# Deferring ten tiles' output products of a sparse graph attention kernel past its last q, k, v product, with deeper gathers and layer norm's small steps on VectorE

## The chip, the cores and the metric

The kernel runs on one core of a Trainium2 chip. Times are device microseconds of that core. Each is one run of the whole program, and runs are compared by their medians.

## The reference

There are 16 graphs (B) of 1024 nodes with 512 features, float32, and one adjacency matrix of 1024 x 1024 zeros and ones for all of them. Node degrees are very uneven: the first nodes have up to some tens of neighbours, the last ones few.

```python
q = (x @ Wq + bq).reshape(b, n, H, HD)     # H = 8 heads of HD = 64
k = (x @ Wk + bk).reshape(b, n, H, HD)
v = (x @ Wv + bv).reshape(b, n, H, HD)
scores = jnp.einsum('bqhd,bkhd->bhqk', q, k) / jnp.sqrt(jnp.float32(HD))
scores = scores + (1.0 - adj)[None, None, :, :] * -1000000000.0
attn = jax.nn.softmax(scores, axis=-1)
out = jnp.einsum('bhqk,bkhd->bqhd', attn, v).reshape(b, n, d)
y = x + out @ Wo + bo
return (y - mean(y)) / sqrt(var(y) + 1e-5)
```

## The kernel before

The kernel uses that the matrix is sparse. Once, at the start, it turns the adjacency matrix into lists of edges (`edges`). A tile is 128 query nodes of one graph, so there are 8 tiles in a graph and 128 in all. For each tile the edges are cut into blocks of 128 pairs of a query and a key. The first OWN[t] blocks hold one neighbour for each of the tile's queries, and the remaining BLOCKS[t] blocks hold the surplus edges of the queries with many neighbours. That makes 12, 5, 4, 3, 3, 3, 3, 3 blocks for tiles 0 to 7, 36 for a graph (NB) and 576 in the whole run. A tile is written (b, t) below: (13, 0) is tile 0 of graph 13.

There are three kinds of work.

1. *Products of q, k, v* (called `fronts` in the code): x is loaded and transposed, and `pair` makes q (L465) and k, v (L581, with seven products for the four quadrants of two tiles), which go to DRAM tables of rows, `q_rows` and `kv_rows`. A last row holds the mean of v. When it is written, the graph counts as set up (L531).
2. *Blocks of attention.* `gather` fetches, with indirect DMAs that GpSimd issues, the k and v rows of a block's keys (L695), and for a surplus block its q rows too (L690). For the other blocks q comes with one load for each tile (L684). VectorE multiplies q and k (L712) and adds up over each head (L716), ScalarE takes the exponential (L726), and ScalarE (L736) or VectorE (L740) weighs v. Own blocks are added up by VectorE (L752), surplus blocks by TensorE with a 0/1 matrix (L761, L762). `normalise` divides (L768 to L775), TensorE transposes the result (L780) and ScalarE copies it to oT (L784).
3. *Finishing a tile.* `load_y` loads x again into y (L637), two turns later GpSimd adds bo (L638), `product` multiplies oT by Wo on TensorE (L465, "po"), and VectorE adds it to y with a row sum (L647). Layer norm follows: a centre step on VectorE (L650), the square sum on ScalarE (L654), scale, power and shift on GpSimd (L657 to L659), and the normalised y on ScalarE (L662) with the store (L663).

All engines run their instructions in the order in which this loop writes them. One turn n of the loop is one block: gathers are issued for block n + 8 (AHEAD, L867), L712 and L716 for block n + 4, the exponential for n + 3, weighing for n + 1 or n + 2, sums for n. `later(k, fn)` puts a step k turns on, `later_last` the same at the end of that turn. TensorE's long work is rationed: every turn earns a `share` of its time (L862, computed once for each graph), every product unit costs its PRODUCT = 0.86 us, and units are taken while credit is positive, `finishing` before `fronts` (L893 to L900). A tile is finished when more than LAZY = 2 tiles wait while fronts are left, and at once afterwards, with at most one tile in two turns. With this the products of q, k, v are used up in turn 526, and from there to turn 576 only blocks and finishing remain. Fifty turns and the drain behind them make the end of the run.

SP issues all plain loads and stores in the order of the loop, so that a store which waits for its y holds up the loads behind it. A buffer that is used again makes its next load wait until the old content has been stored. y has four buffers.

`guard` (L795) starts at turn 540. It tests whether the edge lists and the size of the scores allow this method. Three powers on GpSimd (L817 to L819) come in it, then a few steps on VectorE (L821 to L826), whose result decides at the end of the run whether a dense routine (`tile_general`) has to run. With these inputs it doesn't.

Of the kernel before, what the change touches and what calls it, by code (L numbers as in the profile page):

```python
# [9 lines left out]
F32 = mybir.dt.float32  # L10
# [3 lines left out]
OP = mybir.AluOpType  # L14
# [3 lines left out]
EPS = 1e-5  # L18
# [9 lines left out]
AHEAD = 8  # L28
KG_BUFS, QG_BUFS, QT_BUFS, PV_BUFS = 8, 4, 3, 5
NO_ROW = 65536.0  # L30

LAZY = 2

ROWS = 3
EARLY = 11
LEAD_IN = 34
# [3 lines left out]
SUM = 0.87  # L40
TRANSPOSE = 0.44
LEAD_SHARE = 3.45

P = 128

# [102 lines left out]
def kernel(  # L148
# [34 lines left out]
    nc = tc.nc  # L183
    B, N, D = x.shape
    HD = D // HEADS
    NPAIR = D // P
    NT = N // P
# [4 lines left out]
    NS = sum(BLOCKS)  # L192
    NB = NS + sum(OWN)
# [11 lines left out]
    bo_bc = const.tile([P, D], F32, name="bo_bc")  # L205
# [8 lines left out]
    with ExitStack() as main:  # L214
        one = main.enter_context(tc.tile_pool(name="one", bufs=1))
        work = main.enter_context(tc.tile_pool(name="work", bufs=1))
        small = main.enter_context(tc.tile_pool(name="small", bufs=4))
        psum = main.enter_context(tc.tile_pool(name="psum", bufs=1, space=bass.MemoryType.PSUM))
        dram = main.enter_context(tc.tile_pool(name="dram", bufs=1, space=bass.MemoryType.DRAM))
# [34 lines left out]

        kv_rows = [dram.tile([N + 1, 2 * D], F32, name=f"kv_rows_{i}") for i in range(ROWS)]
        q_rows = [dram.tile([N, D], F32, name=f"q_rows_{i}") for i in range(ROWS)]
        zero = work.tile([1, D], F32, tag="q", name="zero", bufs=2)
        nc.gpsimd.memset(zero, 0.0)
        bias_rows = one.tile([2 * NPAIR, P], F32, name="bias_rows")
# [163 lines left out]
        X, XT, SX, KV, VSUM, NRM, Y, OT, PS = {}, {}, {}, {}, {}, {}, {}, {}, {}  # L423
        set_up = {}
# [206 lines left out]

        loaded = {}

        def load_y(b, t):
            Y[b, t] = work.tile([P, D], F32, tag="y", name=f"y_{b}_{t}", bufs=4)
            loaded[b, t] = now[0]
            nc.sync.dma_start(Y[b, t], x[b, ds(t * P, P), :])  # L637
            later(2, lambda: nc.gpsimd.tensor_tensor(Y[b, t], Y[b, t], bo_bc, op=OP.add))  # L638

        def finish(b, t):  # L640

            def out(p):
                OT.pop((b, t))
                y = Y[b, t]

                st = small.tile([P, 5], F32, name="stats", bufs=6)
                nc.vector.scalar_tensor_tensor(y, p, 1.0, y, op0=OP.mult, op1=OP.add, accum_out=st[:, 0:1])  # L647

                def centre():
                    nc.vector.tensor_scalar(st[:, 1:2], st[:, 0:1], -1.0 / D, None, op0=OP.mult)  # L650

                def spread():
                    sq = work.tile([P, D], F32, tag="ysq", name=f"ysq_{b}_{t}", bufs=1)
                    nc.scalar.activation(sq, y, AF.Square, bias=st[:, 1:2], accum_out=st[:, 2:3])  # L654

                def root():
                    nc.gpsimd.tensor_scalar(st[:, 2:3], st[:, 2:3], 1.0 / D, EPS, op0=OP.mult, op1=OP.add)  # L657
                    nc.gpsimd.tensor_tensor(st[:, 3:4], st[:, 2:3], neg_half, op=OP.pow)  # L658
                    nc.gpsimd.tensor_tensor(st[:, 4:5], st[:, 3:4], st[:, 1:2], op=OP.mult)  # L659

                def norm_out():
                    nc.scalar.activation(y, y, AF.Identity, bias=st[:, 4:5], scale=st[:, 3:4])  # L662
                    nc.sync.dma_start(out_ap[b, ds(t * P, P), :], y)  # L663
                    del Y[b, t]

                later(1, centre)
                later_last(1, spread)
                later(2, root)
                later_last(4, norm_out)

            out_ap = out_dram
            return product(f"po_{b}_{t}", lambda: OT[b, t], W["o"], out)


# [5 lines left out]
        def gather(n):  # L680
            b, t, i = blocks[n]
            if i == 0:
                QT[b, t] = work.tile([P, D], F32, tag="qt", name=f"qt_{b}_{t}", bufs=QT_BUFS)
                nc.sync.dma_start(QT[b, t], q_rows[b % ROWS][ds(t * P, P), :])  # L684
            if i < OWN[t]:
                g = NS + own[t] + i
            else:
                g = first[t] + i - OWN[t]
                QG[n] = work.tile([P, D], F32, tag="qg", name=f"qg_{n}", bufs=QG_BUFS)
# [4 lines left out]
            KG[n] = work.tile([P, 2 * D], F32, tag="kvg", name=f"kvg_{n}", bufs=KG_BUFS)  # L694
# [69 lines left out]
        def normalise(b, t):  # L764
            s, pv = PSUM.pop((b, t)), PV.pop((b, t))
            o = work.tile([P, D], F32, tag="o", name=f"o_{b}_{t}", bufs=2)
            r = small.tile([P, HEADS], F32, tag="rden", name=f"rden_{b}_{t}", bufs=2)
            nc.vector.tensor_tensor(r, s[:, 1, HD2:HD2 + HEADS], pv[:, D:], op=OP.add)  # L768
            nc.vector.tensor_tensor(  # L769
                o.rearrange("p (a d) -> p a d", a=2), s[:, :, 0:HD2], pv[:, 0:D].rearrange("p (a d) -> p a d", a=2),  # L770
                op=OP.add,
            )
            nc.vector.reciprocal(r, r)
            o8 = o.rearrange("p (h d) -> p h d", d=HD)
            nc.vector.tensor_tensor(o8, o8, r[:, :, None].to_broadcast([P, HEADS, HD]), op=OP.mult)  # L775

            def transpose():
                p = fill_psum(f"poT_{b}_{t}")
                for c in range(NPAIR):
                    nc.tensor.transpose(p[:, ts(c, P)], o[:, ts(c, P)], ident)  # L780

                def out():
                    OT[b, t] = work.tile([P, D], F32, tag="oT", name=f"oT_{b}_{t}", bufs=LAZY + 2)
                    nc.scalar.copy(OT[b, t], p)  # L784
                    later(1, lambda: done.append((b, t)))

                later(1, out)

            later(1, lambda: urgent.append(transpose))
            if not fronts:  # L790
                coming.append((b, t))
# [3 lines left out]
        def guard():  # L795
# [15 lines left out]
            r = small.tile([1, 8], F32, name="r")  # L811
            nc.vector.tensor_copy(r[:, 0:4], pg[0:1, 0:4])
            yield

            half = neg_half[0:1, 0:1]
            for i in (0, 1, 3):
                nc.gpsimd.tensor_scalar(r[:, i:i + 1], r[:, i:i + 1], 1e-30, None, op0=OP.max)  # L817
                nc.gpsimd.tensor_tensor(r[:, 4 + i:5 + i], r[:, i:i + 1], half, op=OP.pow)
                nc.gpsimd.tensor_tensor(r[:, i:i + 1], r[:, i:i + 1], r[:, 4 + i:5 + i], op=OP.mult)  # L819
            yield  # L820
            nc.vector.tensor_tensor(r[:, 4:5], r[:, 1:2], r[:, 3:4], op=OP.add)  # L821
            nc.vector.tensor_tensor(r[:, 4:5], r[:, 4:5], r[:, 0:1], op=OP.mult)
# [6 lines left out]
        done, coming, gathered, fronts = [], [], [0], []  # L829

        for i in range(KG_BUFS):
            nc.gpsimd.memset(work.tile([P, 2 * D], F32, tag="kvg", name=f"kvg_first_{i}", bufs=KG_BUFS), 0.0)
# [4 lines left out]
            prep.setdefault(EDGES_FROM[t], []).append(edges(t))  # L837
        prep.setdefault(12 - LEAD_IN, []).append(bias_setup())
        preps = [loads()]
        prep.setdefault((B - 1) * NB, []).append(guard())  # L840
        with tc.manual_schedule():

            fronts += transpose_x(0, 0) + transpose_x(0, 1)
# [5 lines left out]
            finishing, last_finish = [], -LEAD_IN  # L849
            credit = 0.0  # L850
            for t in range(3):
                load_x(0, t)
            n = -LEAD_IN
            while n < total or plan or rest or urgent or done or finishing:
                now[0] = n
                if n < 0:
                    share = LEAD_SHARE if n > -LEAD_IN else TRANSPOSE * 1.5
                elif n % NB == 0:

                    left = sum(u[0] for u in fronts)  # L860
                    goal = fronts_time - (n // NB + 2 + EARLY / NB) * batch_time
                    share = (max(0.0, left - goal) + NT * NPAIR * PRODUCT + NS * SUM) / NB  # L862
                if 0 <= n + 3 < total:
                    exponentials(n + 3)
                if 0 <= n + 4 < total:
                    products(n + 4)
# [87 lines left out]
```

## Time and profile before

| | us |
|---|---|
| median of 3 runs | 2127.69 |
| lowest, highest | 2127.08, 2128.05 |
| the profiled execution | 2129.36 |
| its span in the trace | 2127.5 |
| busy in the span: TensorE | 2038.1 (96%) |
| VectorE | 1850.6 (87%) |
| ScalarE | 1642.1 (77%) |
| GpSimd | 1278.5 (60%) |

The span is the time from the first to the last instruction of one profiled execution. An engine's busy time is the time in which at least one of its instructions was running. PE is TensorE's matmuls, PEld its weight loads, DVE VectorE, ACT ScalarE, POOL GpSimd and SP the engine that issues plain transfers. PEclk is the share of its full clock that TensorE was granted, and DMA the mean busy share of the 16 DMA engines. In a list of waits a line such as "DVE y L647 <- POOL y L638: 10.0, 5, 3.0" says that VectorE stood 10.0 us in all, 5 times, at most 3.0 us, before the instructions of L647, and that GpSimd's L638 ended most of it. The name "po<-wo,oT" gives what is written and what is read.

### The profile page before, as it was taken

The page shows a single profiled execution, that of the slowest core. Times are in us where ns is not written, and L with a number is a line of the kernel's source. Part 1 is how long each engine was busy: PE and PEld are TensorE (multiplying, and loading weights), DVE is VectorE, ACT ScalarE, POOL GpSimd, SP SyncE. Part 2 cuts the span into 40 slices and gives each one's busy share as a digit, 9 for nine tenths or more (in the row PEclk, how much of TensorE's full clock was granted, in tenths as well). Part 3 has the DMA queues.
Part 4 walks back from the last instruction along what each step waited for, and adds up shares of the span by engine and source line. Part 5 has one row for each costly group of instructions (what it writes and reads, how often), then busy time and mean ns, then how long its engine had stood idle before and what let it go on. Part 6 is the DMA issues. An engine that isn't in the chain of part 4 may idle for free. (4 is left out here: it accounts for less than half of the span.)

```text
span 2127.5 us, 29475 instructions
## 1 busy us (share of the span) xinstructions
PE 2038.1 (96%) x5933; PEld 1034.5 (49%) x5933; DVE 1850.6 (87%) x3592; ACT 1642.1 (77%) x8132; POOL 1278.5 (60%) x1366
## 2 busy tenths in 40 slices
PE   8897999999999999999999999999999999999746
PEld 3444555554555555455555545555554555545323
DVE  6789999988888888888898889988889888898866
ACT  4577887878878687787868788786878868697755
POOL 2034576756657575665756566575656656565775
PEclk9998999999999999999999999999999999999859
DMA  5267788887879788787978879787887879788774
GB/s 193 100 242 239 261 292 314 299 299 262 319 242 335 262 275 310 269 305 253 314 269 276 312 252 327 251 314 271 278 308 256 323 246 318 267 276 283 239 257 159
DMA packets 216716, 578.00 MB, mean 272 GB/s; under 512 B 33727, under 2 KB 33739, under 8 KB 216526
## 3 DMA queue, kind: packets, MB, share of 16 engines
q0 software_dynamic: 102144, 331.89, 46.7%
q1 hardware_dynamic: 111776, 239.16, 31.1%
q10 hardware_dynamic: 2606, 4.99, 0.7%
q14 instruction: 141, 1.16, 0.2%
q8 instruction: 49, 0.80, 0.2%
HBM read 474.75 MB, written 134.26 MB: 286 GB/s over the span
## 5 line engine op out<-in xcount | busy, mean ns | idle before, releaser
L695 POOL DMA_INDIRECT kvg<-kv_rows,key_row x576 | 629.5, 1093 | 395.2 <-ACT pv L726 109.9
L736 ACT ACTIVATE pv<-kvg,pv 128x64 f32<-128x64 f32 x2624 | 660.6, 338 | 0.0
L465 PE MATMUL pq<-wq,xT 128*128 128x512 f32 x1024 | 481.3, 595 | 0.0
L465 PE MATMUL po<-wo,oT 128*128 128x512 f32 x1024 | 471.9, 601 | 5.2 <-ACT oT L784 5.2
L716 DVE TENSOR_REDUCE s<-qk 128x8 f32<-128x512 f32 x576 | 391.3, 679 | 6.6
L690 POOL DMA_INDIRECT qg<-q_rows,query_row x240 | 274.7, 1144 | 76.7 <-issue 61.5
L465 PEld LDWEIGHTS po<-wo,oT 128*128 128x128 f32 x1024 | 196.2, 193 | 228.2 <-issue 206.7
L465 PEld LDWEIGHTS pq<-wq,xT 128*128 128x128 f32 x1024 | 189.6, 191 | 193.6 <-issue 178.8
L477 ACT ACTIVATE sq<-q 128x64 f32<-128x64 f32 x1024 | 245.5, 244 | 18.5 <-DVE q L492 18.3
L477 ACT ACTIVATE sq<-kv 128x64 f32<-128x64 f32 x1024 | 245.1, 243 | 1.0 <-DVE kv L604 0.6
L712 DVE TENSOR_TENSOR qk<-qt,kvg 128x512 f32<-128x512 f32 x336 | 243.7, 725 | 0.0
L581 PE MATMUL x<-b,xT 128*128 128x512 f32 x504 | 238.5, 596 | 0.1
L581 PE MATMUL pp<-t,s 128*128 128x512 f32 x504 | 237.2, 593 | 0.7 <-DVE w L597 0.7
L638 POOL TENSOR_TENSOR y<-y,bo_bc 128x512 f32<-128x512 f32 x128 | 173.2, 1353 | 100.0 <-DMA y<-in_x_dram 99.1
L477 ACT ACTIVATION_READ_ACCUMULATOR sq<-q 128x1 f32 x1024 | 195.1, 190 | 0.0
L477 ACT ACTIVATION_READ_ACCUMULATOR sq<-kv 128x1 f32 x1024 | 194.6, 190 | 0.0
L712 DVE TENSOR_TENSOR qk<-qg,kvg 128x512 f32<-128x512 f32 x240 | 173.8, 724 | 19.0 <-DMA kvg<-kv_rows,key_row 18.2
L761 PE MATMUL sum<-pv,sums 128*128 128x256 f32 x480 | 148.5, 392 | 26.1 <-DVE pv L740 23.5
L740 DVE TENSOR_TENSOR pv<-kvg,pv 128x512 f32<-128x512 f32 x248 | 170.5, 688 | 2.0 <-ACT pv L726 1.0
L726 ACT ACTIVATE pv<-s,absent 128x8 f32<-128x8 f32 x336 | 95.0, 292 | 94.8 <-DVE o L769 73.8
L647 DVE SCALAR_TENSOR_TENSOR y<-po,y 128x512 f32<-128x512 f32 x128 | 87.6, 684 | 81.4 <-POOL y L638 66.3
L761 PEld LDWEIGHTS sum<-pv,sums 128*128 128x128 f32 x480 | 91.3, 194 | 134.8 <-issue 99.6
(144 smaller groups left out, 3009.8 us busy)
## 6 DMA issues: line engine op xcount, KB each, us to landing
kv_rows<-kv SPq DMA_DIRECT2D x128, 512.0 KB
x<-in_x_dram SPq DMA_DIRECT2D x128, 256.0 KB
q_rows<-q SPq DMA_DIRECT2D x128, 256.0 KB
qt<-q_rows SPq DMA_DIRECT2D x128, 256.0 KB
y<-in_x_dram SPq DMA_DIRECT2D x128, 256.0 KB
out_dram<-y SPq DMA_DIRECT2D x128, 256.0 KB
kvg<-kv_rows,key_row POOLq DMA_INDIRECT x576
a<-in_adj_dram SPq DMA_DIRECT2D x8, 512.0 KB
```

The source lines that it names most:

```text
L465: nc.tensor.matmul(p, lhs()[:, ts(c, P)], w[:, c, :], start=(c == 0), stop=(c == NPAIR - 1))
L477: nc.scalar.activation(sq, s[:, ts(h, HD)], AF.Square, accum_out=NRM[b][:, i, t, h:h + 1])
L581: nc.tensor.matmul(R[bank], l[:, ts(c, P)], right[:, c, :], start=(first and c == 0), stop=(c == 1), skip_group_check=True,)
L638: later(2, lambda: nc.gpsimd.tensor_tensor(Y[b, t], Y[b, t], bo_bc, op=OP.add))
L690: nc.gpsimd.indirect_dma_start(out=QG[n], out_offset=None, in_=q_rows[b % ROWS], in_offset=bass.IndirectOffsetOnAxis(ap=query_row[:, g:g + ...
L695: nc.gpsimd.indirect_dma_start(out=KG[n], out_offset=None, in_=kv_rows[b % ROWS], in_offset=bass.IndirectOffsetOnAxis(ap=key_row[:, g:g + ...
L712: nc.vector.tensor_tensor(QK[n], q, KG[n][:, 0:D], op=OP.mult)
L716: nc.vector.tensor_reduce(S[n], QK.pop(n).rearrange("p (h d) -> p h d", d=HD), axis=AX.X, op=OP.add)
L726: nc.scalar.activation(PV[n][:, D:], S.pop(n), AF.Exp, bias=bias)
L736: nc.scalar.activation(pv[:, ts(h, HD)], v[:, ds(D + h * HD, HD)], AF.Copy, scale=pv[:, D + h:D + h + 1])
L740: nc.vector.tensor_tensor(pv[:, 0:D].rearrange("p (h d) -> p h d", d=HD), v[:, D:].rearrange("p (h d) -> p h d", d=HD), pv[:, D:, None].to ...
L761: nc.tensor.matmul(PSUM[b, t][:, 0, 0:HD2], m, pv[:, 0:HD2], **kw)
```

## The change

- The ten tiles (12, 6) to (13, 7), numbers 102 to 111, aren't finished in their turn. Their oT is stored to DRAM (`spill`). From the time that no `fronts` are left they are read back one after the other, at most two of them with a y at a time and at least three turns apart, into the buffers "e", "w", "g" of the q, k, v products, with y in the buffers "q".
- From graph 13 on, the share is computed anew in every turn so that the fronts end at turn 526 (EARLY and 3 turns before graph 15), and it is 3.0 after them.
- After the fronts gathers run 11 blocks ahead instead of 8. Every second q and k, v gather, and q of the even tiles, then take buffers that the fronts have left ("x", "xT", "kv").
- Layer norm's scale step (`variance`) and `shift` go from GpSimd to VectorE, for all tiles. The power stays on GpSimd, and shift comes a turn later.
- y + bo of even tiles goes to VectorE for tiles loaded after the fronts.
- The guard starts four turns earlier and leaves more turns between its steps.

```diff
+SPILL = range(102, 112)
+AHEAD_LAST = 11
+LAST_SHARE = 3.0
...
-        def load_y(b, t):
-            Y[b, t] = work.tile([P, D], F32, tag="y", name=f"y_{b}_{t}", bufs=4)
+        def load_y(b, t, tag="y", bufs=4):
+            Y[b, t] = work.tile([P, D], F32, tag=tag, name=f"y_{b}_{t}", bufs=bufs)
             loaded[b, t] = now[0]
             nc.sync.dma_start(Y[b, t], x[b, ds(t * P, P), :])
-            later(2, lambda: nc.gpsimd.tensor_tensor(Y[b, t], Y[b, t], bo_bc, op=OP.add))
+            engine = nc.gpsimd if fronts or t % 2 else nc.vector
+            later(2, lambda: engine.tensor_tensor(Y[b, t], Y[b, t], bo_bc, op=OP.add))
+
+        def reload(b, t, k):
+            OT[b, t] = work.tile([P, D], F32, tag="ewg"[k % 3], name=f"oTs_{b}_{t}", bufs=1)
+            nc.sync.dma_start(OT[b, t], spill[b * NT + t - SPILL[0]])
+            load_y(b, t, "q", 2)
+            later(2, lambda: done.append((b, t)))
...
-                def root():
-                    nc.gpsimd.tensor_scalar(st[:, 2:3], st[:, 2:3], 1.0 / D, EPS, op0=OP.mult, op1=OP.add)
+                def variance():
+                    nc.vector.tensor_scalar(st[:, 2:3], st[:, 2:3], 1.0 / D, EPS, op0=OP.mult, op1=OP.add)
                     nc.gpsimd.tensor_tensor(st[:, 3:4], st[:, 2:3], neg_half, op=OP.pow)
-                    nc.gpsimd.tensor_tensor(st[:, 4:5], st[:, 3:4], st[:, 1:2], op=OP.mult)
+
+                def shift():
+                    nc.vector.tensor_tensor(st[:, 4:5], st[:, 3:4], st[:, 1:2], op=OP.mult)
...
-                later(2, root)
+                later(2, variance)
+                later(3, shift)
                 later_last(4, norm_out)
...
-                QT[b, t] = work.tile([P, D], F32, tag="qt", name=f"qt_{b}_{t}", bufs=QT_BUFS)
+                tag, bufs = ("qt", QT_BUFS) if fronts or t % 2 else ("x", 3)
+                QT[b, t] = work.tile([P, D], F32, tag=tag, name=f"qt_{b}_{t}", bufs=bufs)
...
+                tag, bufs = ("qg", QG_BUFS) if fronts or i % 2 else ("xT", 4)
...
+            tag, bufs = ("kvg", KG_BUFS) if fronts or n % 5 % 2 == 0 else ("kv", 5)
...
                     nc.scalar.copy(OT[b, t], p)
-                    later(1, lambda: done.append((b, t)))
+                    if b * NT + t in SPILL:
+                        nc.sync.dma_start(spill[b * NT + t - SPILL[0]], OT.pop((b, t)))
+                        spilled.append((b, t))
+                    else:
+                        later(1, lambda: done.append((b, t)))
...
-        prep.setdefault((B - 1) * NB, []).append(guard())
+        prep.setdefault((B - 1) * NB - 4, []).append(guard())
...
+            fronts_end = (B - 1) * NB - EARLY - 3
...
+                elif n >= SPILL[0] // NT * NB + NB:
+
+                    share = sum(u[0] for u in fronts) / max(fronts_end - n, 1) + NS * SUM / NB if fronts else LAST_SHARE
...
-                while gathered[0] < min(n + AHEAD + 1, total) and blocks[gathered[0]][0] in set_up:
+                while gathered[0] < min(n + (AHEAD if fronts else AHEAD_LAST) + 1, total) and blocks[gathered[0]][0] in set_up:
...
-                    if tile_done not in loaded and len(Y) < 4:
+                    if tile_done not in loaded and sum(b * NT + t not in SPILL for b, t in Y) < 4:
                         load_y(*tile_done)
...
+                if spilled and not fronts and n > last_reload + 2 and sum(b * NT + t in SPILL for b, t in Y) < 2:
+                    reload(*spilled.pop(0), reloads)
+                    reloads, last_reload = reloads + 1, n
```

More of the change, by code (lines that the diff above doesn't have):

```diff
@@ L256 @@
         q_rows = [dram.tile([N, D], F32, name=f"q_rows_{i}") for i in range(ROWS)]
+        spill = [dram.tile([P, D], F32, name=f"spill_{i}") for i in range(len(SPILL))]
         zero = work.tile([1, D], F32, tag="q", name="zero", bufs=2)
@@ L688, in gather @@
                 g = first[t] + i - OWN[t]
-                QG[n] = work.tile([P, D], F32, tag="qg", name=f"qg_{n}", bufs=QG_BUFS)
+                tag, bufs = ("qg", QG_BUFS) if fronts or i % 2 else ("xT", 4)
+                QG[n] = work.tile([P, D], F32, tag=tag, name=f"qg_{n}", bufs=bufs)
                 nc.gpsimd.indirect_dma_start(
@@ L693, in gather @@
                 )
-            KG[n] = work.tile([P, 2 * D], F32, tag="kvg", name=f"kvg_{n}", bufs=KG_BUFS)
+            tag, bufs = ("kvg", KG_BUFS) if fronts or n % 5 % 2 == 0 else ("kv", 5)
+            KG[n] = work.tile([P, 2 * D], F32, tag=tag, name=f"kvg_{n}", bufs=bufs)
             nc.gpsimd.indirect_dma_start(
@@ L813, in guard @@
             yield
+            yield
             half = neg_half[0:1, 0:1]
@@ L819, in guard @@
                 nc.gpsimd.tensor_tensor(r[:, i:i + 1], r[:, i:i + 1], r[:, 4 + i:5 + i], op=OP.mult)
+            yield
+            yield
             yield
@@ L828 @@
         out_dram = out
-        done, coming, gathered, fronts = [], [], [0], []
+        done, coming, spilled, gathered, fronts = [], [], [], [0], []
         for i in range(KG_BUFS):
@@ L848 @@
             batch_time = fronts_time / B
-            finishing, last_finish = [], -LEAD_IN
+            finishing, last_finish, reloads, last_reload = [], -LEAD_IN, 0, 0
+            fronts_end = (B - 1) * NB - EARLY - 3
             credit = 0.0
@@ L853 @@
             n = -LEAD_IN
-            while n < total or plan or rest or urgent or done or finishing:
+            while n < total or plan or rest or urgent or done or finishing or spilled:
                 now[0] = n
```

## The prediction

> **What bounds the kernel now.** I read the busy row of the page first, then busy time by stretch, then who waits for whom in the stretches that the change touches, then single instructions there. I cut the span at VectorE's products of queries and keys (L712), because each of the 576 blocks has exactly one, written four turns ahead: turn 468 (first of batch 13) starts at 1761.1 us, turn 526 at 1958.7, turn 571 at 2100.6.
>
> ```profile
> PE   8897999999999999999999999999999999999746
> DVE  6789999988888888888898889988889888898866
> ```
>
> TensorE is full in nearly every slice and drops only in the last three. The stretches, with columns length, busy time of PE, PEld, DVE, ACT, POOL, granted clock, DMA share, GB/s:
>
> ```profile
> core 0: us, PE busy (x) PEld busy (x) DVE busy (x) ACT busy (x) POOL busy (x), PEclk, DMA share, GB/s
> ...
> 159.00:500.00 341.00, 328.45 (x963) 168.81 (x964) 320.73 (x633) 274.79 (x1361) 209.18 (x216) 0.97 0.83 283
> 500.00:1761.10 1261.10, 1260.55 (x3712) 643.00 (x3711) 1110.82 (x2129) 1008.51 (x5096) 792.09 (x842) 1.00 0.82 285
> 1761.10:1958.70 197.60, 197.60 (x576) 100.63 (x575) 175.42 (x329) 162.36 (x826) 123.88 (x133) 1.00 0.83 287
> 1958.70:2100.60 141.90, 93.90 (x246) 47.56 (x244) 112.11 (x226) 90.44 (x351) 104.83 (x121) 0.80 0.74 249
> 2100.60:2127.50 26.90, 14.52 (x44) 6.98 (x44) 10.87 (x27) 12.10 (x33) 8.34 (x15) 0.86 0.20 72
> ```
>
> Up to 1958.7 us TensorE is the bound: 197.60 busy of 197.60, with VectorE second at 89%. I call 1761.1 to 1958.7 stretch A. In 1958.7 to 2100.6 (stretch B) the products of q, k, v have run out, no engine is full, and TensorE idles 48 us. The last 26.9 us (C) drain. VectorE's waits in B:
>
> ```profile
> DVE y L647 <- POOL y L638: 10.0, 5, 3.0
> DVE qk L712 <- DMA kvg<-kv_rows,key_row: 8.6, 3, 4.1
> DVE r L821 <- POOL r L819: 6.0, 1, 6.0
> DVE y L647 <- issue: 2.6, 1, 2.6
> ```
>
> These are 27 of its 29.8 us of idle time: the addition of po waits for GpSimd's y + bo, gathers land late, and the guard waits for three powers on GpSimd. The chain that ended last covers only the last microseconds (statistics, y, store) and says nothing about A or B.
>
> **What the Trainium skill says.** "TensorE: Matmul & The Clock Gate", What's actually happening: the clock is throttled by default and activity releases it. The trace agrees. Eight po matmul records in a full stretch, and eight after idling in B:
>
> ```profile
> 1966.66 3.60 PE L465 MATMUL po<-wo,oT 128*128 128x512 f32 x8
> 1970.10 0.60 PE L761 MATMUL sum<-pv,sums 128*128 128x256 f32 x2
> ...
> 2004.62 6.78 PE L465 MATMUL po<-wo,oT 128*128 128x512 f32 x8 [1.00 <-ACT oT L784]
> ```
>
> "DMA: Bandwidth & Descriptors", Anatomy of one DMA — SWDGE (gpsimd) path: DMA engines don't wait on semaphores, the issuing sequencer does, and a transfer has about 2 us of fixed cost (measured there on the gpsimd path). Here SP indeed stands 51.5 us in B before output stores that wait for ScalarE's y, and a y load takes 2.7 us from issue to use when the DMA is idle (2106.3 to 2109.0) but 6.0 when it isn't (1997.3 to 2003.3). "SBUF — State Buffer", SBUF: two separate sides: a VectorE operation with two SBUF inputs and a GpSimd operation that reads SBUF exclude each other. The trace agrees: L712 at 1977.32 took 2.40 us instead of 0.68 while a y + bo ran on GpSimd.
>
> **Part 1: ten output products leave A.** The ten tiles (12,6) to (13,7) no longer get their product with Wo in A. One product is the eight records above: 1970.10 - 1966.66 = 3.44 us, so ten are 34.4 us, and A's TensorE time falls from 197.6 to 163.2. The products of q, k, v end in turn 525 either way, since the new share is made for that. VectorE loses ten additions (0.61 from start to next) and ten centre steps (0.06): 6.7 us, leaving 168.7. So VectorE takes over as the bound of A. ScalarE loses 10 x 1.5 us (147 left), GpSimd ten y + bo and statistics. DMA: 0.83 x 197.6 = 164 us of full use; ten y loads and ten stores go, ten spill stores come, 2.6 MB less of 56.7, so 156.5, or 0.90 of 174. Single windows of 12.4 us show 0.95 at 354 GB/s, so I take it as hidden; if not, A keeps a few us. To 168.7 I add waits. Before, VectorE waited 15.7 us in A for TensorE's products; with TensorE no longer full I keep a third, 5.3. A = 174.0, with ends 169 (no wait kept) and 184 (all 15.7 kept). Gain 23.6. The spill's store waits on SP for ScalarE's copy of oT; queued behind it are q, kv and x transfers, but the copy is issued in the same turn, so nothing is added; if ScalarE lagged a turn, the 3 us fall on transfers with several turns in hand.
>
> **Part 2: they come back in B.** In the built order of instructions, VectorE gets from turn 526 to 571: 9 more additions of po (0.61), 11 y + bo for even tiles (0.60 as L712 is spaced), 30 more small scalar steps and 21 shifts (0.06 to 0.08 each): 5.5 + 6.6 + 3.3 = 15.4, so 127.5 busy. With full single durations it would be 133. TensorE gets 9 x 3.4 = 31 us: 125, some of it at the lower clock, which should now rise as gaps close. DMA gets a spill read, a y load and a store for nine tiles, 6.9 MB on 35.3: 0.74 x 141.9 = 105 becomes 126. GpSimd stays near 104: more powers, but fewer y + bo and two small steps less for each tile. Three resources within 3% of each other don't all stay full, so B is VectorE's work plus waits:
> - guard: starts four turns earlier with four more turns of room, 6.0 to 0;
> - gathers: 11 ahead where the key row is used four turns early, so seven turns of lead for four, at some 3 us each. That is 21 us for 12, against an issue-to-use time that ran short at 5 to 8 us. 8.6 becomes 2. The first must still wait for the mean's row, as before;
> - y + bo on GpSimd, odd tiles only: 12.6 becomes 4;
> - new: VectorE itself waits for the y load of even tiles, with the next qk and the products with v queued behind, and TensorE's sums behind those. GpSimd waited 10.3 us in B for 13 loads, 0.8 each; VectorE reaches the place 2.2 to 5.9 us after the load's issue in turns 525 to 540, and up to 4 us before a landing of 6.0, but later has 6.8 us and more. Bounds 0 and 3.5 each; I take 1.3, so 11 x 1.3 = 14.
> B = 127.5 + 0 + 2 + 4 + 14 = 147.5, 5.6 more than before. SP's reloads of oT into the e, w, g buffers wait for the product of three reloads before, long done.
>
> **Part 3: layer norm's small steps on VectorE, all 128 tiles.** Up to 1761.1 they cost 100 x 2 x 0.07 = 14 us of VectorE, which has 150 us idle after 500 alone: hidden by TensorE. The wait counts more. `variance` waits for ScalarE's square sum, `shift` for GpSimd's power. Putting each where the new order has it between the instructions of the old trace, VectorE would arrive too early 33 times in the first 100 tiles, 52.7 us in total, at most 2.7, and 12.4 us for `shift`. Behind it stand scores and evacuations. But TensorE starts its sums at least 1.9 us after VectorE's weighting ends and the transpose of o at least 1.75 after o; only the part above 1.75, 7.1 us in total, could reach it, and VectorE already has waits of 2.95 us in this stretch with TensorE full. I take 1 us; ends -1 (GpSimd is freed) and 7. In C the chain gets two crossings between engines for two same-engine steps (POOL to POOL was 0.04 to 0.08), one more addition and 13 small steps: 28.0 for 26.9.
>
> **The sum.** 1761.1 + 1 + 174.0 + 147.5 + 28.0 = 2111.6 us of span against 2127.5: 15.9 less. The profiled execution took 2129.36, 1.9 more than its span, and lies 1.7 above the median of 2127.69, so I subtract from the median: 2111.8.
>
> **The rivals.**
> - *Both stretches at VectorE's rate.* Waits shrink once gathers lead: A 171, B 127.5 + 8 = 135.5, C 27.5, nothing before: 2095.1, so 2095.3. For it: VectorE already ran at 94% beside TensorE's 96% from 159 to 500. Against: DMA above 0.9 in both.
> - *Slower: VectorE held up by y's load.* Mechanism: y + bo of even tiles in B, in order on VectorE, behind a load that SP issues only after a store waiting for ScalarE. If each waits 3.5 us (6.0 to landing less 2.5 to arrival, as at tiles (14,4) and (14,6)), B grows by 11 x 2.2 = 24: 2136. It turns the sign from 1.3 + 15.9/11 = 2.75 us a tile. Against: most arrivals before came later than 4 us after issue.
> - *Given back, no change: layer norm's waits reach TensorE.* If a quarter of the 65 us of `variance` and `shift` waits passed on, 16 us go: 2128. Against: the lead of 1.75 us and more.
> - *The change not doing what it says* is excluded for the order: built, 40 po matmuls read reloaded tiles, after the last product of q.
>
> **How the numbers follow.** Chances: my forecast with its own 2103 to 2121, 0.62; fast case 0.20; layer norm's waits 0.08; slower case 0.10. Predicted is the likeliest, 2111.8. The range goes from 2094, just below the fast case, to 2126, near A's upper end (10 more) and some more waits, leaving the slower cases out. A measurement of this kernel tells about 0.2% (4.3 us) from none. Faster 0.82, same 0.08, slower 0.10.
>
> **What would show it.** After: L712 of turn 468 within 3 us of 1761; from there to that of turn 526 about 174 us with TensorE at some 163 and VectorE above 95%; no guard wait; waits of VectorE for y's load of some 14 us in B and hardly any for gathers. TensorE with gaps between 500 and 1761, waiting for pv or o, would make part 3 wrong; A still near 197, or B above 163, parts 1 and 2.

## The result and the profile after

| | before | after | forecast |
|---|---|---|---|
| median (lowest, highest), us | 2127.87 (2127.08, 2130.59), 4 runs | 2132.41 (2129.98, 2133.13), 4 runs | 2111.8 |
| the profiled execution | 2129.36 | 2129.98 | |
| its span | 2127.5 | 2128.1 | 2111.6 |
| start to turn 468 | 1761.1 | 1766.1 | 1762.1 |
| A, turns 468 to 526 | 197.6 | 169.7 | 174.0 |
| B, turns 526 to 571 | 141.9 | 162.7 | 147.5 |
| C, drain | 26.9 | 29.6 | 28.0 |

The ratio is 1.0017, interval 1.0000 to 1.0034: no change, or a little slower. The 28 us that A lost came back, 20.8 in B, 2.7 in C and 5.0 before turn 468. From the page of the kernel after, the busy tenths in 40 slices:

```profile
PE   8997999999999999999999999999999999998676
DVE  6889999999889999988999999998999989998777
```

TensorE now drops over the last four slices instead of three, and VectorE shows more nines before that. The same five stretches of the kernel after, cut at its own product of queries and keys (L731):

```profile
core 0: us, PE busy (x) PEld busy (x) DVE busy (x) ACT busy (x) POOL busy (x), PEclk, DMA share, GB/s
159.00:500.00 341.00, 325.44 (x958) 166.22 (x957) 322.77 (x661) 272.60 (x1348) 199.26 (x180) 0.98 0.82 281
500.00:1766.10 1266.10, 1262.53 (x3714) 642.99 (x3713) 1162.06 (x2295) 1008.65 (x5101) 735.53 (x678) 1.00 0.82 284
1766.10:1935.80 169.70, 165.73 (x498) 84.94 (x497) 164.00 (x304) 148.89 (x799) 106.14 (x91) 1.00 0.92 321
1935.80:2098.50 162.70, 118.29 (x318) 58.46 (x316) 129.97 (x305) 100.72 (x371) 97.62 (x101) 0.90 0.76 259
2098.50:2128.10 29.60, 17.84 (x52) 8.58 (x52) 14.67 (x44) 14.96 (x38) 6.21 (x8) 0.88 0.27 93
```

A is now held by two engines: TensorE busy 165.7 and VectorE 164.0 of 169.7. B is held by none. VectorE, the busiest, works 130.0 us and stands 32.7, and the DMA share is only 0.76. In the two stretches up to turn 468, where TensorE is the bound, it idles 15.56 + 3.57 = 19.1 us, where it idled 12.55 + 0.55 = 13.1 before. VectorE's longest waits in B:

```profile
DVE y L645 <- DMA y<-in_x_dram: 17.3, 6, 4.2
DVE stats L674 <- POOL stats L671: 5.9, 2, 5.6
DVE y L660 <- POOL y L645: 4.8, 1, 4.8
```

The first is the addition of bo waiting for the load of y, the second layer norm's `shift` waiting for GpSimd's power. The gather waits (8.6) and the guard's (6.0) are gone. SP's queue in the same stretch shows why y is late:

```profile
SPq L678 <- ACT pv L745: 42.5, 8, 10.7
SPq L642 <- DMA out_dram<-y: 35.2, 12, 4.0
SPq L678 <- ACT y L677: 34.3, 8, 8.0
```

L678 is the store of a finished y, L642 the load of the next. SP stands before the store until ScalarE has made y (L677; for part of these waits the profile names the exponential, L745, which ScalarE runs close to it), and then before the load until a store has emptied the load's buffer. Some of it in order of time:

```profile
1973.09 0.34 SPq L678 DMA_DIRECT2D out_dram<-y  x1
1977.21 0.33 SPq L642 DMA_DIRECT2D y<-in_x_dram  x1
1977.97 0.34 SPq L678 DMA_DIRECT2D out_dram<-y  x1
1978.37 0.42 SPq L649 DMA_DIRECT2D oTs<-spill  x1
1981.25 0.33 SPq L642 DMA_DIRECT2D y<-in_x_dram  x1
```

These two loads leave SP 4.1 and 3.3 us after the store ahead of them. VectorE has to wait for the second, until 4.4 us after its issue at 1981.25:

```profile
1985.68 0.69 DVE L645 TENSOR_TENSOR y<-y,bo_bc 128x512 f32<-128x512 f32 x1 [3.07 <-DMA y<-in_x_dram]
```

### The profile page after: what moved, and what is told of

Its sections match the earlier page's. It is cut to its first block, busy times and chain, and to the rows that moved or that the text cites. A ratio compares the mean times of both kernels' runs of the same rounds, so it can differ in the third digit from the quotient of the medians.

```text
span 2128.1 us, 29503 instructions
## 1 busy us (share of the span) xinstructions
PE 2035.1 (96%) x5933; PEld 1030.2 (48%) x5933; DVE 1915.1 (90%) x3860; ACT 1640.7 (77%) x8132; POOL 1185.5 (56%) x1098
## 5 line engine op out<-in xcount | busy, mean ns | idle before, releaser
L714 POOL DMA_INDIRECT kvg<-kv_rows,key_row x576 | 642.3, 1115 | 398.3 <-DVE pv L759 131.2
L470 PE MATMUL po<-wo,oT 128*128 128x512 f32 x944 | 430.3, 595 | 0.7 <-ACT oT L803 0.7
L708 POOL DMA_INDIRECT qg<-q_rows,query_row x240 | 265.6, 1107 | 76.7 <-issue 63.4
L470 PEld LDWEIGHTS po<-wo,oT 128*128 128x128 f32 x944 | 179.1, 191 | 200.8 <-issue 185.9
L731 DVE TENSOR_TENSOR qk<-qt,kvg 128x512 f32<-128x512 f32 x336 | 241.3, 718 | 0.2 <-issue 0.2
L671 POOL TENSOR_TENSOR stats<-stats,neg_half 128x1 f32<-128x1 f32 x128 | 88.1, 688 | 262.1 <-DVE stats L670 255.7
L645 POOL TENSOR_TENSOR y<-y,bo_bc 128x512 f32<-128x512 f32 x116 | 158.2, 1364 | 103.4 <-DMA y<-in_x_dram 98.8
L745 ACT ACTIVATE pv<-s,absent 128x8 f32<-128x8 f32 x336 | 95.9, 292 | 112.0 <-DVE o L788 73.3
L731 DVE TENSOR_TENSOR qk<-qg,kvg 128x512 f32<-128x512 f32 x240 | 176.3, 735 | 2.0 <-DMA kvg<-kv_rows,key_row 1.5
L771 DVE TENSOR_TENSOR pv<-pv,pv 128x520 f32<-128x520 f32 x208 | 175.7, 845 | 0.1
```

The costliest lines, as they stand in the source:

```text
L470: nc.tensor.matmul(p, lhs()[:, ts(c, P)], w[:, c, :], start=(c == 0), stop=(c == NPAIR - 1))
L645: later(2, lambda: engine.tensor_tensor(Y[b, t], Y[b, t], bo_bc, op=OP.add))
L708: nc.gpsimd.indirect_dma_start(out=QG[n], out_offset=None, in_=q_rows[b % ROWS], in_offset=bass.IndirectOffsetOnAxis(ap=query_row[:, g:g + ...
L714: nc.gpsimd.indirect_dma_start(out=KG[n], out_offset=None, in_=kv_rows[b % ROWS], in_offset=bass.IndirectOffsetOnAxis(ap=key_row[:, g:g + ...
L731: nc.vector.tensor_tensor(QK[n], q, KG[n][:, 0:D], op=OP.mult)
L771: nc.vector.tensor_tensor(PV[b, t], PV[b, t], pv, op=OP.add)
```

## The experiments

Theory: the deferral does in A what was forecast, and B gives it back because y's loads leave SP late; separately, layer norm's steps on VectorE make it wait, and that reaches TensorE before turn 468. Rivals: the engine that adds bo, the burst of gathers, or the mere number of VectorE's instructions. "Before" had medians of 2128.8 to 2129.6 in these comparisons. The segments are of each run's profiled execution.

| run | median us | ratio, interval | to turn 468 | A | B | C |
|---|---|---|---|---|---|---|
| e1_bias | 2133.17 | 1.0022, 1.0014 to 1.0030 | 1769.4 | 170.3 | 164.1 | 29.7 |
| e2_ln | 2124.20 | 0.9978, 0.9969 to 0.9987 | 1760.7 | 171.8 | 161.2 | 29.8 |
| e3_spill | 2122.51 | 0.9971, 0.9961 to 0.9980 | 1760.1 | 170.1 | 160.5 | 29.8 |
| e4_bufs | 2122.77 | 0.9969, 0.9960 to 0.9978 | 1768.0 | 170.2 | 153.8 | 29.6 |
| e5_lnonly | 2134.78 | 1.0025, 1.0016 to 1.0033 | 1766.0 | 198.2 | 142.9 | 26.4 |
| e7_ahead8 | 2131.77 | 1.0014, 1.0007 to 1.0021 | 1765.1 | 172.2 | 163.2 | 29.7 |
| e8_lnlater | 2132.37 | 1.0014, 1.0007 to 1.0020 | 1763.7 | 198.2 | 140.9 | 26.7 |
| e9_ln_bufs | 2122.00 | 0.9963, 0.9949 to 0.9976 | 1762.3 | 171.0 | 156.9 | 29.7 |
| e10_ln_bufs_store | 2117.32 | 0.9946, 0.9932 to 0.9960 | 1759.0 | 171.3 | 156.3 | 29.7 |
| e11_hybrid | 2109.82 | 0.9918, 0.9905 to 0.9930 | 1761.5 | 170.1 | 145.7 | 29.6 |
| e12_ramp | 2105.32 | 0.9892, 0.9878 to 0.9906 | 1760.7 | 170.2 | 141.9 | 29.6 |
| e13_five | 2130.09 | 1.0003, 0.9995 to 1.0011 | 1764.9 | 185.5 | 147.8 | 26.4 |
| e14_idle | 2128.90 | 0.9999, 0.9992 to 1.0005 | 1761.6 | 197.2 | 142.8 | 27.0 |
| e15_ramp | 2130.61 | 1.0005, 0.9997 to 1.0013 | 1765.5 | 171.5 | 160.7 | 29.6 |
| e16_keep | 2115.30 | 0.9930, 0.9917 to 0.9944 | 1759.8 | 198.5 | 129.3 | 26.9 |
| e17_nine | 2103.93 | 0.9883, 0.9867 to 0.9898 | 1760.8 | 170.1 | 143.9 | 29.3 |
| e18_var | 2130.68 | 1.0006, 0.9998 to 1.0015 | 1765.5 | 197.4 | 139.1 | 27.0 |

**Which engine adds bo.** After, with GpSimd adding it for all tiles:

```diff
-            engine = nc.gpsimd if fronts or t % 2 else nc.vector
+            engine = nc.gpsimd
```

> The changed kernel with one part undone: y + bo of all tiles stays on GpSimd. Theory 1 (VectorE held up by y's load: it stood 17.3 us in stretch B for y's DMA): those 17.3 us leave VectorE, some 5 come back as waits for GpSimd's y + bo, so about 2132 - 10 = 2122. Theory 2 (the ten tiles' work fills the end of the run and waits only change places): the same time within 4 us, with the waits now listed as y<-po behind GpSimd's y. Theory 3 (layer norm's steps): no change, 2132.

2133.17 us, B 164.1: no difference from after that these runs can tell. The wait only changed its place. GpSimd in B:

```profile
POOL y L645 <- DMA y<-in_x_dram: 12.7, 6, 6.3
```

and VectorE stands behind GpSimd instead (L660 <- POOL y, 8.4 us). So here it made no difference which engine waits for y; that y is late remains.

**The late loads.** After, with a fifth buffer for y and a third place for deferred y's:

```diff
-        def load_y(b, t, tag="y", bufs=4):
+        def load_y(b, t, tag="y", bufs=5):
...
-            load_y(b, t, "q", 2)
+            load_y(b, t, *(("q", 2) if k % 3 < 2 else ("vsum", 1)))
```

> The changed kernel with one more buffer for y of the ordinary tiles and one more for the deferred ones, so that most y loads no longer wait for the store issued just ahead of them. Theory 1: SP's wait for stores (35.2 us in B, 12 times) goes nearly, VectorE's wait for y's load of 17.3 us falls to 5 or less, and the time to about 2120. Theory 2: 2130 to 2133, the loads are early and nothing else moves. Theory 3: 2132.

2122.77 us, some 10 less than after, and B is 8.9 us shorter. VectorE's wait for y in B and SP's two longest waits there:

```profile
DVE y L645 <- DMA y<-in_x_dram: 9.9, 4, 4.2
```

```profile
SPq L678 <- ACT pv L745: 72.5, 11, 12.5
SPq L678 <- ACT y L677: 41.7, 10, 7.2
```

The line with "out_dram<-y" is no longer in SP's list, and VectorE's wait for y fell from 17.3 to 9.9. So loads that are late through store and buffer cost B some 9 us, more than any other single repair takes from it (e15 2.0, e2 1.5, e1 and e7 nothing). The Trainium skill, "DMA: Bandwidth & Descriptors", Anatomy of one DMA — SWDGE (gpsimd) path, puts the wait in the issuing sequencer. The trace agrees: here that is SP, which stood 35.2 us before loads in B of after, with all its later transfers behind them.

**Layer norm's steps.** After with scale and shift back on GpSimd, before with these two alone on VectorE, and before with these a turn later:

```diff
e2_ln, after:
-                    nc.vector.tensor_scalar(st[:, 2:3], st[:, 2:3], 1.0 / D, EPS, op0=OP.mult, op1=OP.add)
+                    nc.gpsimd.tensor_scalar(st[:, 2:3], st[:, 2:3], 1.0 / D, EPS, op0=OP.mult, op1=OP.add)
...
-                    nc.vector.tensor_tensor(st[:, 4:5], st[:, 3:4], st[:, 1:2], op=OP.mult)
+                    nc.gpsimd.tensor_tensor(st[:, 4:5], st[:, 3:4], st[:, 1:2], op=OP.mult)
e5_lnonly, before: the same two lines from gpsimd to vector, shift at later(3)
e8_lnlater, as e5:
-                later(2, variance)
-                later(3, shift)
-                later_last(4, norm_out)
+                later(3, variance)
+                later(4, shift)
+                later_last(5, norm_out)
```

> The changed kernel with layer norm's scale and shift back on GpSimd. Theory 3 (layer norm's steps on VectorE are the loss): the first 1766 us become 5 shorter, the 5.9 us that VectorE stood for GpSimd's power in B go, and VectorE has 42 instructions less there: 2132 - 12 = 2120. Theories 1 and 2: at most the early 5 us, so 2127 to 2132.

> The kernel before with layer norm's scale and shift on VectorE alone, nothing else changed. If these steps are what makes the first 1766 us longer: turn 468 comes 5 to 9 us later and the time is 2134 to 2138 against 2128.8. If that loss needs the rest of the change: 2128 to 2130.

> As e5_lnonly, with scale, shift and output one turn later each, so that ScalarE's square sum and GpSimd's power have a turn more to be ready. If VectorE's waits for them (28 us for the sum between 500 and 1766 us) are the loss: it goes, 2128 to 2130. If it is the 256 added instructions on VectorE, where it is nearly full (159 to 500 us): as slow as e5_lnonly, within 2 us.

e2 is 8 us faster than after, e5 6.0 slower than before, e8 3.6 slower. The largest wait of VectorE from 500 us to 1766 us in e5:

```profile
DVE stats L657 <- ACT ysq L654: 28.4, 22, 2.7
```

Over all kernels shown, those with both steps on GpSimd up to there (ten, before among them) reach turn 468 at 1759.0 to 1762.3 us, mean 1760.8; those with both on VectorE in their first place (seven, after among them) at 1764.9 to 1769.4, mean 1766.4. The groups don't overlap: 5.6 us. Kernels that do the same up to there differ by up to 4.5 us, though (e13 1764.9, e1 1769.4), nearly all of it in the first 500 us. From the product of queries and keys at some 501 us (block 108) to turn 468 the ten take 1258.8 to 1260.4 us and the seven 1262.4 to 1263.0, 3.2 more in the mean, and TensorE idles 0.3 to 0.9 us there in the ten and 2.9 to 3.6 in the seven. TensorE's longest wait there in after, and within 0.1 us in all seven, is this (in e5 it is L465 behind L647); none of the ten has it:

```profile
PE pq L470 <- DVE y L660: 2.3, 2, 1.4
```

One of the two, with VectorE's steps ahead of it:

```profile
907.22 0.15 DVE L670 TENSOR_SCALAR stats<-stats 128x1 f32<-128x1 f32 x1 [2.69 <-ACT ysq L667]
912.67 0.67 DVE L660 SCALAR_TENSOR_TENSOR y<-po,y 128x512 f32<-128x512 f32 x1
913.41 1.13 PE L470 MATMUL pq<-wq,xT 128*128 128x512 f32 x2 [0.89 <-DVE y L660]
```

VectorE stands 2.69 us for the square sum and then works without a pause until it adds a finished po to y (L660). The product of q needs one of the four accumulators (`fill`) that such products and the transposes share, so it waits until VectorE has read po out of one. That is how a wait on VectorE reaches TensorE.

Whether instructions or waits cost this was asked with two unread VectorE instructions for each tile, which wait for no other engine:

```diff
+                later(2, lambda: nc.vector.tensor_scalar(st[:, 5:6], st[:, 1:2], 1.0 / D, EPS, op0=OP.mult, op1=OP.add))
...
+                later(3, lambda: nc.vector.tensor_tensor(st[:, 6:7], st[:, 1:2], st[:, 1:2], op=OP.mult))
```

> The kernel before, with two added 128x1 operations on VectorE for each finished tile, at the places of scale and shift, that read only VectorE's own centre value and whose results nobody reads; layer norm itself stays on GpSimd. If 256 more instructions on VectorE are the loss that e5_lnonly shows (6.0 us, of which 3.6 stayed with a turn more of room): 3 to 4 us more than before, about 2132. If it is all waiting: 2129 within 1 us.

No difference: 2128.90. So the instructions by themselves cost nothing, and waiting is what is left. It isn't the amount of waiting. From 500 us to turn 468 VectorE waited longer in before than in after:

```profile
DVE y L647 <- POOL y L638: 48.8, 31, 4.0
```

In after that wait for GpSimd's y + bo is 7.5, and VectorE idles 104 us there instead of 150. Nor is it the square sum alone: e8 has no such wait left in that stretch, yet 3.6 of the 6.0 us stay, and TensorE still idles 2.3 us there. Which of the two crossings costs more was asked of before with `variance` alone on VectorE:

```diff
-                    nc.gpsimd.tensor_scalar(st[:, 2:3], st[:, 2:3], 1.0 / D, EPS, op0=OP.mult, op1=OP.add)
+                    nc.vector.tensor_scalar(st[:, 2:3], st[:, 2:3], 1.0 / D, EPS, op0=OP.mult, op1=OP.add)
```

> The kernel before with the scale step of layer norm (variance) alone on VectorE, power and shift left on GpSimd as before. With both on VectorE it was 2134.8, 6.0 us slower than before; with both a turn later 3.6 slower; with two small steps that wait for no other engine 0.1. Theory 'the wait for ScalarE's square sum': between 500 us and 1766 us VectorE stood 28.4 us before variance and less than 2 before shift, so variance alone costs 5 to 6 us: 2133.5 to 2135. Rival 'the wait for GpSimd's power, or the turn by which shift comes later': variance alone costs 0 to 2 us: 2128.5 to 2131.

The median, 2130.68, lies in the rival's band, but the place is the theory's. Turn 468 comes at 1765.5, 4.4 us later than before and as late as with both steps, and B is 2.8 us shorter (VectorE's wait for GpSimd's y + bo is 4.0 there instead of 10.0). So far as this one profiled execution can show it, `variance` with its wait for ScalarE's square sum makes the loss before turn 468. The second crossing, `shift`, costs e5 another 4 us in total (the intervals of e5 and e18 don't overlap). It lies in B, 142.9 against 139.1, where VectorE in e5 waits for GpSimd's power:

```profile
DVE stats L661 <- POOL stats L658: 6.7, 3, 4.7
```

That this wait is the whole of it isn't shown.

**The deferral alone, and half of it.** e3 is before with only the spill, the reload and the share of the change; e13 is after with five deferred tiles:

```diff
e3_spill, against after:
-AHEAD_LAST = 11
+AHEAD_LAST = 8
...
-            engine = nc.gpsimd if fronts or t % 2 else nc.vector
+            engine = nc.gpsimd
...
-        prep.setdefault((B - 1) * NB - 4, []).append(guard())
+        prep.setdefault((B - 1) * NB, []).append(guard())
with scale and shift on GpSimd, and the gathers in their own buffers
e13_five, against after:
-SPILL = range(102, 112)
+SPILL = range(107, 112)
```

> The kernel before with the deferral of ten tiles alone: y + bo and layer norm's steps on GpSimd, gathers 8 ahead in their own buffers, the guard where it was. If the deferral by itself gains (A some 28 us shorter, B less than that longer): 2110 to 2120. If the end of the run cannot take ten more tiles (theory 2): 2128 or more, since the late gathers and the guard's 6 us are added to it.

> The changed kernel with only the last five of the ten tiles deferred. A becomes some 13 us longer than with ten. If each tile costs B what the ten did on average (20.9/10 = 2.1 us), B is 10 us shorter: 2132.5 + 13 - 10 = 2136. If B fills up only with the last of them (its resources near full), it falls by 15 us or more: 2130 or less.

Alone the deferral gains 6.3 us. Against before, the first five tiles (e13) take 12.1 us from A and put 5.9 into B; the next five (after against e13) take 15.8 from A and put 14.9 into B and 3.2 into C. In these profiles the second five return more than they gain; the medians, 2130.09 and 2132.41, have intervals that overlap, so as a whole the second five are not told from none. The price of a tile brought back need not be constant, but the two fives aren't a clean comparison: against before, e13 also has the rest of the change, which takes waits out of B, so its five tiles may cost more than 5.9.

**The gathers' lead.** After with 8 blocks ahead in the gathers' own buffers (e7), and after with a lead that grows from 8 to 11 by a block every three turns instead of at once (e15):

```diff
e7_ahead8:
-AHEAD_LAST = 11
+AHEAD_LAST = 8
and the buffers "x", "xT", "kv" not used for gathers
e15_ramp:
-                while gathered[0] < min(n + (AHEAD if fronts else AHEAD_LAST) + 1, total) and blocks[gathered[0]][0] in set_up:
+                while gathered[0] < min(n + (AHEAD if fronts else min(AHEAD_LAST, AHEAD + (n - fronts_end) // 3)) + 1, total) and blocks[gathered[0]][0] in set_up:
```

> The changed kernel with gathers 8 ahead in their own buffers to the end. If the gathers 11 ahead save what the prediction says (VectorE's 8.6 us of waits for gathers): 2132.5 + 6, so about 2138. If the burst of four blocks' gathers in turn 526, when the last kv stores, the first reload and y loads are queued too, costs about as much (y's load came 4.2 us late there): turns 526 to 531 fall from 24 to 20 us, gathers are waited for later, and the time is within 3 us of 2132.

> The changed kernel with the gathers' lead growing from 8 to 11 over nine turns, nothing else. If the burst of gathers at turn 526 costs by itself what it cost in e11_hybrid (4.5 us): 2128. If y loads that wait for stores come late anyway and hide it: 2131 to 2133, as with 8 ahead to the end (2131.8).

Neither differs from after by more than 2 us. The deeper lead is worth nothing here. It isn't even what took the gather waits away: with a lead of 8, VectorE in B of e7 waits for no gather either, and for y's load 15.8 us. B is as long without it.

**Repairs on top of each other.** e9 is after with e2 and e4 together. e10 puts the output stores after the fronts on ScalarE's queue. e11 takes layer norm's steps back to VectorE, but only for tiles finished after the fronts. e12 adds e15's gradual lead:

```diff
e10_ln_bufs_store:
-                    nc.sync.dma_start(out_ap[b, ds(t * P, P), :], y)
+                    (nc.sync if fronts else nc.scalar).dma_start(out_ap[b, ds(t * P, P), :], y)
e11_hybrid, in place of nc.gpsimd in variance and shift:
+                ln = nc.gpsimd if fronts else nc.vector
...
+                later(2 if ln is nc.gpsimd else 3, shift)
```

> The changed kernel with layer norm's steps back on GpSimd and one more y buffer for each kind of tile: both repairs at once. If they are independent losses (8.5 and 10 us): 2132.5 - 18.5 = 2114. If both act on the same waits of the end of the run: 2119 to 2122, no better than one.

> As e9_ln_bufs, and after the last q, k, v product the output stores are issued by ScalarE itself behind its y, not by SP. If SP standing before stores (some 100 us in B, with y, q and oT loads behind them) is what still delays y: B some 5 us shorter, about 2110. If ScalarE's issue time or the DMA queues are what counts: the same as e9_ln_bufs or up to 3 us more.

> As e10_ln_bufs_store, but layer norm's scale and shift go to VectorE for tiles finished after the last q, k, v product (GpSimd before that). If GpSimd's load in B (115 us and the wait for the guard of 3 to 5 us) is what these steps relieve, and their cost lies only in the 100 tiles before: B some 3 us shorter than e10_ln_bufs_store, 2114. If VectorE's own work sets B: 3 us longer, 2120.

> As e11_hybrid, with the gathers' lead growing from 8 to 11 by one block in three turns from turn 526 on. If the burst at turn 526 delays the first y loads (7.9 us of VectorE's time in e10_ln_bufs_store): turns 526 to 531 fall from 28 to about 21 us, and the time to 2108 to 2110. If those loads are late for another reason (kv stores and the mean's row ahead of them on SP): the same as e11_hybrid.

e9 is hardly better than e2 or e4 alone: with the steps back on GpSimd, VectorE in B waits 4.9 us for the guard's steps on GpSimd again and 15.7 for y's load, where e4 had 9.9. e10's median is 4.7 us lower, but its profiled execution wins 3.3 of its 3.8 us before turn 468, where nothing was changed, so that gain isn't put down to the stores. e11 is clear. Stretch B of e10:

```profile
1930.30:2086.60 156.30, 121.07 (x318) 58.92 (x317) 123.85 (x263) 101.95 (x371) 115.07 (x143) 0.89 0.80 275
```

and of e11:

```profile
1931.60:2077.30 145.70, 118.13 (x318) 59.21 (x316) 130.15 (x305) 102.05 (x371) 100.25 (x102) 0.89 0.84 295
```

GpSimd sheds 14.8 us, VectorE takes 6.3 on, and B is 10.6 us shorter. So the same steps hurt on VectorE before turn 468, where TensorE is full, and help in B, where GpSimd is loaded. e12 gains 4.5 more: the burst of gathers at turn 526 delayed the first y load (7.0 us of wait in e11, 3.5 in e12). In after, whose loads were late anyway, the same edit (e15) gave 1.8, within what these runs can't tell. Stretches A and B of e12:

```profile
1760.70:1930.90 170.20, 165.95 (x499) 85.21 (x498) 163.42 (x299) 148.66 (x799) 104.38 (x94) 1.00 0.91 319
1930.90:2072.80 141.90, 116.28 (x318) 58.31 (x316) 129.77 (x304) 101.88 (x371) 101.45 (x102) 0.92 0.85 303
```

B has the same work as in after (VectorE busy 129.8 and 130.0 us), done in 20.8 us less, with the DMA at 303 GB/s instead of 259. SP's wait does not tell this: in e12 it is longer than ever.

```profile
SPq L642 <- DMA out_dram<-y: 106.3, 12, 18.2
```

With no stores in its queue SP reaches each load early and stands there until the buffer is free; VectorE waits 3.5 us in all for y. A long wait is harmless where nothing that is needed stands behind it.

**What the deferral is worth then, and nine tiles.** e16 is e12 without deferred tiles and with the old share, e17 is e12 with nine:

```diff
e16_keep:
-SPILL = range(102, 112)
+SPILL = range(128, 138)
...
-                elif n >= SPILL[0] // NT * NB + NB:
-
-                    share = sum(u[0] for u in fronts) / max(fronts_end - n, 1) + NS * SUM / NB if fronts else LAST_SHARE
e17_nine:
-SPILL = range(102, 112)
+SPILL = range(103, 112)
```

> e12_ramp without the deferral: all 128 tiles finished in their turn, with the added y buffers, the stores from ScalarE, the late layer norm on VectorE and the gathers' slow lead. If the deferral is what wins in e12_ramp (A some 27 us shorter, B and C some 14 longer than they would be): about 2118. If the repairs win and the deferral gives its gain back: 2105 to 2108.

> The best version so far (2105.3 us) with nine tiles deferred, (12,7) to (13,7), instead of ten. With ten tiles four output products lie behind the last product of queries and keys, with none and with five deferred only three, and that drain takes 29.6 us instead of 26.4 to 26.9. Theory 'one tile more in the drain': tiles are finished at most every second turn, so with nine the backlog is empty one tile earlier, the drain has three products and falls to 26.5, and the stretch up to turn 526 grows by 2.8 us (a tenth of 28); in all about even, 2104 to 2107. Rival 'the drain is slow because of what it runs (layer norm across two engines)': four products or not, it stays at 29 to 30 us, and the time goes to 2107 to 2109.

e16 takes 2115.30 us: the repairs gain 13.5 us without any deferral. Deferral on top of them gains 10.0 (e12): A -28.3, B +12.6, C +2.7. e17, 2103.93, is the lowest, but its interval and e12's overlap. It speaks against the theory of one tile more in the drain. With ten tiles four output products lie behind the last product of queries and keys, with nine three, as in before, and C still takes 29.3 us, now with a product that waits 1.99 us for oT and takes 5.40 us (the mean granted clock of the stretch is 0.82). Why C is 3 us longer stays open.

## Why the prediction was wrong

The misses add up: +4.0 before turn 468, -4.3 in A, +15.2 in B, +1.6 in C, together 16.5 of span.

- *Part 1 (A) was right in the main.* The ten products leave, and VectorE comes level with TensorE, though it doesn't take over as the bound. TensorE 165.7 for 163.2 forecast, VectorE 164.0 for 168.7, idle VectorE 5.7 for the 5.3 that I kept. That VectorE lost 11.4 us of work and not 6.7 is why A came out below the forecast. e3 shows that the deferral alone does it, A 170.1.
- *Part 2 (B) failed at its sum,* "B = 127.5 + 0 + 2 + 4 + 14 = 147.5". By term: VectorE's busy time 130.0 (+2.5); guard 0, right; gathers about 0 (-2); y + bo on GpSimd 4.8 (+0.8); y's load on VectorE 17.3 (+3.3); layer norm's wait for GpSimd's power, 5.9, which I had not put there at all; and 4.7 in short waits and gaps (among them for TensorE's products) that the sum had no place for, though before had 2.6 of them. The y term looks nearly right by luck: 14 was 11 waits of 1.3 us, and it was 6 of 2.9. Its cause was bigger than its line: e4 takes 8.9 us from B by making loads earlier. The step that failed is its price, by old distances between VectorE and the load's issue, "later has 6.8 us and more". With two tiles in flight and one store in front of each load, those distances shrank over the whole of B (4.2 us of wait at 1954, and 4.2 again at 2045). The reloads of oT, put at nothing, came late twice in the same queue, both times issued right behind a store:

```profile
PE po L470 <- DMA oTs<-spill: 8.5, 2, 5.8
```

- *The term "gathers: 8.6 becomes 2"* came out in size (0), but not by its reason: with the old lead the wait is gone too (e7).
- *Part 3 failed at "I take 1 us".* It was 5.6 between the groups, near the upper end of 7. The step that fell is "only the part above 1.75, 7.1 us in total, could reach it". It looked at two ways to TensorE, its sums and the transpose of o. The waits went by a third, the accumulator of po that the next product of q waits for: 2.3 of the 3.6 us that TensorE idled from 500 us on. From 159 to 500 us TensorE idled 3.0 more than in before, but kernels that do the same up to there differ by twice that (12.2 in e13, 19.0 in e1), so that part stays open. That the instructions themselves are free was right (e14).
- *The slower rival* had the right place, y's load behind a store on SP. Its price, 24 us, was too high as VectorE's wait (17.3), and its carrier, VectorE instead of GpSimd, was wrong: e1 moves the addition to GpSimd and nothing changes. *Given back* had the right mechanism at a third of its price, 5.6 for 16. Each was too small to be the outcome, and I put them as alternatives. Both came, each in part, and with the short waits they took back all that A gave.

## What to carry to other kernels

Work that is moved into a stretch with idle engines is priced by the serial chain it goes through there (load, use, store, buffer free, next load, all issued by one queue), not by the engines' free time: one more buffer for each kind of tile gave 10 us, and ten tiles cost B 12.6 us once the chain was mended (e12 against e16), against 18.6 without any repair (e3 against before). A small step on an in-order engine is priced by what it waits for: two instructions for each tile that wait for nobody cost nothing, two that wait for neighbours 6 us, though VectorE stood longer in all in before. So follow a wait to what it holds up, here an accumulator that TensorE needed, instead of adding up the waits. Waits that seem to be rivals can all come true at once; add them before choosing among them.

## What the runs showed of the hardware

The same DMA engines moved 259 GB/s in B of after and 303 in B of e12 with the same work to do, so a share of 0.76 was not a limit of the DMA. TensorE's mean granted clock in B was 0.80 in before, where it is busy 66% of the time, 0.90 in after (73%) and 0.92 in e12 (82%), but also 0.88 in e16 at 70%, so the busy share alone doesn't give it. In e17's last 40 us eight output matmuls took 3.60 us right behind other matmuls, and 5.40 us after TensorE had stood 1.99 us.
